# One 16 KB read for two 8 KB reads in the stores of full slots

## The chip, the cores and the metric

The kernel runs on one core of one Trainium2 chip. The metric is the device time of one execution in microseconds, taken as the median of several runs; before the change it is 323.96 us (three runs, 323.84 to 323.97).

## The reference

There are 128 examples x[b], each a float32 matrix of 128 rows (c) by 1024 columns (t), and eight 128 x 128 weight matrices. Each example picks one matrix by its subject number, is multiplied by it, and the product is added to the example:

```python
def _L0_cond_ref(x, subjects, weights):
    w = weights[subjects]                      # (128, 128, 128)
    out = jnp.einsum('bct,bcd->bdt', x, w)     # (128, 128, 1024)
    return out
x = x + _L0_cond_ref(x, itok_B_0_7, L0_cond_weights)
```

The input and the output have 67.1 MB each, so that the kernel has to move 134.2 MB between DRAM and SBUF.

## The kernel before

Four examples (G = 2 times H = 2) make one *slot* of 2 MB: in SBUF a slot is 16 KB on each of the 128 partitions, four rows of 4 KB that stand side by side. There are 32 slots of work (NT = 32) and room for 12 of them in SBUF (SLOTS = 12); slot i of the work uses place i mod 12. Two examples, half a slot, are the unit of computing: 64 halves in all.

*Loads.* The ACT queue issues them (L188 to L195): four of 512 KB for each slot, one for each example. On the DRAM side a load takes pieces of 16 KB (ROWS = 4 rows of 4 KB), and on the SBUF side it fills one 4 KB row on each partition. From the thirteenth slot on, ACT first waits at L193 until the stores of the slot that had the same place before have landed.

*Computing.* For each half, POOL copies the two weight matrices that the subjects choose into small tiles (L222), once both loads of the half have landed (the wait at L226). PE makes eight matmuls of 512 columns (L156), and DVE adds the two products, which lie in PSUM, to the two examples in place (L234): the result stands where the input was.

*Stores.* SP issues them (`store`, L140 to L147) after it has waited for the addition of the half (L239). Slot 0 and slot 31 are stored by halves (1 MB each; of the last half one example alone, 512 KB), the thirty slots between them whole, 2 MB in one DMA. The very last example, 512 KB, is stored at L252 by an ordinary DMA, which SP issues last. On the DRAM side a store writes pieces of 4 KB, one row of an example. On the SBUF side a piece is `g` rows: in the kernel before, `g = min(G, q1 - q0)`, so that a whole slot is read in two pieces of 8 KB from each partition.

Loads and stores are in two hardware queues (the profile's q10 for the loads, q1 for the stores, which also has the two small loads at the start) that share the same 16 DMA engines. Each DMA of 128 partitions is spread over all 16. In the trace each queue's work is a row of packets: one for each contiguous piece that is read, and at the end of a DMA one of 4 bytes on each engine, which counts up the DMA's semaphore.

Of the kernel before, what the change touches and what calls it, by code (L numbers as in the profile page):

```python
# [30 lines left out]
G = 2  # L31
# [20 lines left out]
def transfer(nc, engine, out, in_):  # L52

    later, nc._always_lower_symbolic_ap = nc._always_lower_symbolic_ap, False
    ins, outs = engine.lower_ap_dma(in_), engine.lower_ap_dma(out)
    nc._always_lower_symbolic_ap = later
    return engine.add_instruction(
        mybir.InstDMACopy(  # L60
            name=nc.get_next_instruction_name(),
            engine=engine.engine,
            ins=ins,
            outs=outs,
            mode="Copy",
            cce_op=ALU.bypass,
            queue=QUEUES[engine.engine],
        )
    )
# [3 lines left out]
def kernel(  # L73
# [17 lines left out]
    if room:  # L91
        sbuf("room", C, room // 4)
    x_all = sbuf("x_all", C, SLOTS * H * G * T)
    xs = [
        x_all[:, i * H * G * T : (i + 1) * H * G * T].rearrange("c (q t) -> c q t", t=T)
        for i in range(SLOTS)
    ]
# [42 lines left out]
    def store(i, q0, q1):  # L140
        k, b = i % SLOTS, i * H * G
        transfer(
            nc,
            nc.sync,
            out[b + q0 : b + q1].rearrange("g d t -> d g t"),
            xs[k][:, q0:q1, :].rearrange("d (o g) t -> d o (g t)", g=min(G, q1 - q0)),
        ).then_inc(s_first if i == 0 and q1 == G else s_pair[k][(q1 - 1) // G], DMA)  # L147

    def multiply(slot, q0, q1):
# [15 lines left out]
    with tc.tile_critical():  # L165
# [22 lines left out]
        for i in range(NT):  # L188
            k = i % SLOTS
# [8 lines left out]
        for j in range(NT * H):  # L198
            i, q0, q1 = j // H, j % H * G, (j % H + 1) * G
            k = i % SLOTS  # L200
# [37 lines left out]
            if i == 0 or q1 == H * G or i == NT - 1:  # L238
                nc.sync.wait_ge(s_added, j + 1)  # L239
                store(i, q0 if i in (0, NT - 1) else 0, q1 - (b == B - 1))  # L240
# [46 lines left out]
```

## Time and profile before

| what | value |
|---|---|
| median of three runs | 323.96 us |
| the profiled execution's own time | 324.29 us |
| span of that execution, first to last instruction | 322.5 us |
| PE busy | 241.0 us (75%) |
| DVE busy | 147.9 us (46%) |
| POOL busy | 34.0 us (11%) |
| end of the last addition (L234) in the span | 274.8 us |
| moved by the DMA engines | 134.79 MB, mean 418 GB/s |

The busy times are sums over the whole span. No computing engine is busy for more than three quarters of it, and the last addition ends 47.7 us ahead of the span's end. The span and the execution's own time differ by 1.8 us, which lie around the first and the last instruction.

### The profile page before, as it was taken

How to read it: one execution, taken by the hardware profiler on the slowest of the kernel's cores; microseconds unless marked ns; L12 is line 12 of the kernel's file. 1: busy time of each engine (PE TensorE's matmuls, PEld its weight loads, DVE VectorE, ACT ScalarE, POOL GpSimd, SP SyncE). 2: the span in 40 equal slices, each digit the busy share in tenths (PEclk: the TensorE clock that was granted, in tenths of full speed). 3: DMA queues.
4: the chain of work that ended last, by engine and by line, in shares of the span. 5: the costliest groups of instructions: out<-in, count | busy, mean ns of one | idle time of the engine just before them, and what ended most of it. 6: DMA issues, size and time to landing. Idle time of an engine off the chain costs nothing. (4 is left out here: it accounts for less than half of the span.)

```text
span 322.5 us, 2012 instructions
## 1 busy us (share of the span) xinstructions
PE 241.0 (75%) x518; PEld 94.8 (29%) x518; DVE 147.9 (46%) x68; POOL 34.0 (11%) x132
## 2 busy tenths in 40 slices
PE   6999999988988888888888898888887687000000
PEld 2344444333333333333333333333332232000000
DVE  1266665655555555545555555555553554000000
POOL 0011111111111111111111111111111010000000
PEclk9799999999999999999999999999999999655555
DMA  7999999999999999999999999999999999999997
GB/s 240 431 414 431 417 426 434 429 416 429 426 426 426 434 418 428 431 422 426 431 425 424 431 419 428 429 426 424 431 422 424 430 422 427 427 425 427 426 429 296
DMA packets 16070, 134.79 MB, mean 418 GB/s; under 512 B 2625, under 2 KB 3650, under 8 KB 3906
## 3 DMA queue, kind: packets, MB, share of 16 engines
q1 hardware_dynamic: 9922, 67.64, 50.0%
q10 hardware_dynamic: 6144, 67.12, 49.6%
q14 instruction: 4, 0.03, 0.0%
HBM read 67.63 MB, written 67.11 MB: 418 GB/s over the span
## 5 line engine op out<-in xcount | busy, mean ns | idle before, releaser
L156 PE MATMUL ps<-x_all,w 128*128 (+1 forms) x512 | 235.9, 607 | 29.8 <-PEq L152 29.8
L234 DVE TENSOR_TENSOR x_all<-ps,x_all 128x2048 f32<-128x2048 f32 x64 | 146.7, 2292 | 125.1 <-PE ps L156 125.1
L156 PEld LDWEIGHTS ps<-x_all,w 128*128 128x128 f32 x512 | 92.9, 191 | 173.1 <-issue 173.1
L222 POOL COPY w<-w_all 128x128 f32 x128 | 33.8, 293 | 234.2 <-DMA x_all<-in_x_dram 186.2
L173 PE MATMUL ps<-zeros 128*128 128x512 f32 x6 | 5.1, 1020 | 1.7 <-DVE zeros L170 1.7
L173 PEld LDWEIGHTS ps<-zeros 128*128 128x128 f32 x6 | 1.9, 330 | 3.7 <-issue 2.1
L170 DVE MEMSET zeros<- 128x512 f32 x1 | 0.5, 485 | 1.1 <-SPq L165 1.1
L180 DVE TENSOR_SCALAR near<-given 1x128 int32<-1x128 int32 x1 | 0.2, 215 | 0.6 <-DMA given<-in_itok_B_dram 0.6
L184 DVE CUSTOM_DVE_ANT_0 index<-near,wrap 1x256 uint16<-1x256 uint16 x1 | 0.3, 278 | 0.0
L182 DVE TENSOR_SCALAR wrap<-near 1x128 int32<-1x128 int32 x1 | 0.2, 216 | 0.0
L274 POOL MEMSET const-float32-0.0<- 128x1 f32 x1 | 0.1, 98 | 0.2 <-issue 0.2
L274 POOL MEMSET const-bfloat16-1.0<- 128x1 bf16 x1 | 0.1, 101 | 0.0
L274 POOL MEMSET const-uint8-127<- 128x1 uint8 x1 | 0.1, 101 | 0.0
L274 POOL MEMSET const-float32-1.0<- 128x1 f32 x1 | 0.1, 98 | 0.0
## 6 DMA issues: line engine op xcount, KB each, us to landing
x_all<-in_x_dram ACTq DMA_DIRECT2D x128, 512.0 KB, 32.0
out_dram<-x_all SPq DMA_DIRECT2D x30, 2048.0 KB, 48.3
out_dram<-x_all SPq DMA_DIRECT2D x3, 1024.0 KB, 13.5
out_dram<-x_all SPq DMA_DIRECT2D x2, 512.0 KB, 20.6
w_all<-in_L_cond_weights_dram SPq DMA_DIRECT2D x1, 512.0 KB, 6.1
given<-in_itok_B_dram SPq DMA_DIRECT2D x1, 0.5 KB
```

The lines of the kernel that those rows point to most:

```text
L156: mm = nc.tensor.matmul(p[:, q % G, t : t + N], ws[q % W_SLOTS][:, 0, :], x_all[:, bass.ds(at, N)], start=True, stop=True,)
L170: nc.vector.memset(zeros, 0.0).then_inc(s_zeros, 1)
L173: nc.tensor.matmul(ps[P_SLOTS - 1][:, G - 1, :N], zeros[:, :D], zeros, start=True, stop=True)
L180: nc.vector.tensor_scalar(near, given, -S, S - 1, ALU.max, ALU.min).then_inc(s_index, 1)
L182: nc.vector.tensor_scalar(wrap, near, 0, S, ALU.is_lt, ALU.mult).then_inc(s_index, 1)
L184: nc.vector.tensor_tensor(index, near, wrap, ALU.add).then_inc(s_index, 1)
L222: copy = nc.gpsimd.tensor_copy(ws[b % W_SLOTS], w_all[:, bass.ds(subject[b % R], 1), :])
L234: nc.vector.tensor_tensor(mine, p, mine, ALU.add).then_inc(s_added, 1)
L274: nc = _bacc.Bacc("TRN2", target_bir_lowering=False, num_devices=1)
```

## The change

One argument in `store` is changed. Where a store covers a whole slot, q1 - q0 is 4, and the four rows of a partition are now read as one piece of 16 KB; the stores by halves (q1 - q0 = 2) and of one example keep their pieces. The bytes, their order, the 4 KB pieces on the DRAM side, the number of DMAs, the semaphores and the waits stay as they are, and every engine's instructions stand in the same order as before.

```diff
@@ def store(i, q0, q1)
             nc.sync,
             out[b + q0 : b + q1].rearrange("g d t -> d g t"),
-            xs[k][:, q0:q1, :].rearrange("d (o g) t -> d o (g t)", g=min(G, q1 - q0)),
+            xs[k][:, q0:q1, :].rearrange("d (o g) t -> d o (g t)", g=q1 - q0),
         ).then_inc(s_first if i == 0 and q1 == G else s_pair[k][(q1 - 1) // G], DMA)
```

## The prediction

> **What bounds the kernel now.** I read the page's slices first, to find the resource that is full; then its queues; then the DMA view cut to three stretches, to see what one packet costs and how the two queues share the engines; then the end of the timeline. The profile's page:
>
> ```profile
> PE   6999999988988888888888898888887687000000
> ...
> DMA  7999999999999999999999999999999999999997
> ...
> q1 hardware_dynamic: 9922, 67.64, 50.0%
> q10 hardware_dynamic: 6144, 67.12, 49.6%
> ...
> out_dram<-x_all SPq DMA_DIRECT2D x30, 2048.0 KB, 48.3
> ```
>
> The DMA engines are full in every slice but the first and the last; PE stops near slice 34. So the time is that of the bytes. The counts tell what a packet is. A load of 512 KB puts 32 KB on each of 16 engines: two pieces of 16 KB and the 4-byte packet, 3 packets, and 128 x 16 x 3 = 6144. A full slot's store puts 128 KB on an engine: 16 pieces of 8 KB and one of 4 bytes, 17 packets. A store needs 48.3 us to land: the store queue has a backlog.
>
> The three stretches are 10 to 18 us (loads alone), 40 to 240 us (both) and 270 to 315 us (stores alone); columns are packets, MB, share of 16 engines.
>
> ```profile
> DMA packets 309, 3.42 MB, mean 428 GB/s; under 512 B 100, under 2 KB 100, under 8 KB 100
> ...
> q10 hardware_dynamic: 309, 3.42, 100.8%
> ...
> DMA packets 9180, 85.27 MB, mean 426 GB/s; under 512 B 1791, under 2 KB 1791, under 8 KB 1791
> ...
> q10 hardware_dynamic: 4538, 49.47, 58.5%
> q1 hardware_dynamic: 4638, 35.77, 42.5%
> ...
> DMA packets 2489, 19.19 MB, mean 426 GB/s; under 512 B 147, under 2 KB 147, under 8 KB 147
> ...
> q1 hardware_dynamic: 2489, 19.19, 101.3%
> ```
>
> Two things are to be seen. Loads alone, both together and stores alone all run at 426 to 428 GB/s. And while both queues have work they get the same number of packets (4538 and 4638), not of bytes: the engines take turns by packet, and the 4-byte packet takes a turn too. Three turns of loads carry 32 KB, 10.7 KB a turn; 17 turns of stores carry 128 KB, 7.5 KB a turn. That makes 1.42; the bytes above stand 1.38 to 1. So loads run ahead of stores until the 12 places are full, and this lead is stored at the end, long after computing is over:
>
> ```profile
> 267.95 0.53 POOL L222 COPY w<-w_all 128x128 f32 x2 [3.48 <-DMA x_all<-in_x_dram]
> ...
> 272.50 2.29 DVE L234 TENSOR_TENSOR x_all<-ps,x_all 128x2048 f32<-128x2048 f32 x1 [1.67 <-PE ps L156]
> ...
> 301.87 0.37 SPq L252 DMA_DIRECT2D out_dram<-x_all  x1
> ```
>
> The waits of SP's queue (total us, times, longest) have the rest:
>
> ```profile
> SPq L283 <- DMA out_dram<-x_all: 19.2, 1, 19.2
> ```
>
> The last load has landed at 267.9; the half's last addition ends at 274.79, 6.84 us after its weight copy begins at 267.95; SP still has DMAs to wait for at the end, 19.2 us. The computing of the last slot costs nothing now, because from 267.4 us on, where the last load packet ends, the engines still have 54 us of stores to move, 23 MB at 426 GB/s.
>
> **What the change does, part by part.**
>
> *Fewer packets.* The 30 full stores go from 16 to 8 pieces on an engine: 30 x 8 = 240 packets fewer for each engine, 3840 in all. What is one worth? By duration: in the middle stretch a load packet of 16 KB takes (58.5% of 3200 us, less 1519 small ones of 9 ns) / 3019 = 615.5 ns, a store packet of 8 KB (42.5% of 3200 us, less 272 small ones) / 4366 = 310.9 ns; two of these less one of those is 6.3 ns, and 240 x 6.3 = 1.5 us. But durations overlap (the shares are over 100%), so I also take the pace. The semaphore steps of the loads that land from 9.10 to 18.94 us, eight of them, are 1.230 us apart on the mean engine, or 615 ns for 16 KB with its part of the 4-byte packets. Those of the full stores that land alone are 4.918 us apart, 614.7 ns for 16 KB. By that a saving is 0; with 9 ns taken off for each small packet it is 613.6 - 610.5 = 3.1 ns, or 0.75 us. Below nothing: no row has a 16 KB read from SBUF; the slowest stretch of mixed traffic, 245 to 267 us, ran at 423 GB/s for 426, and 63 MB at that pace would be 1.0 us longer. Bounds: 1.0 us lost to 1.5 us gained. I take 0.4 us gained, the middle of the two readings of pace, since these count what passes, not how long a packet is in flight.
>
> The Trainium skill (DMA: Bandwidth & Descriptors, "Why small descriptors are slow (HBM only)") puts some 3 cycles of fixed cost on each packet. By its 850 MHz that is an estimated 3.5 ns, 0.85 us here; the paces above lie below that, and by the page the sum below would be 0.45 us smaller.
>
> *The turns.* A full store is now 9 packets for 128 KB, 14.2 KB a turn, against the loads' 10.7. Where both have work, stores get 57% of 426 GB/s, 244, and loads 183. Stores can't outrun computing, so the store queue runs empty now and then, and loads take what is left: in balance each slot takes 2 x 2.097 MB / 0.426 = 9.84 us, of which its store needs 2.097 / 0.244 = 8.6 us. The early backlog (computing starts at 7.05 us a slot) shrinks by 1.2 us a slot and is gone well before slot 30. The engines stay full: the load queue has work as long as places are free, and the lead is then some 4 to 6 MB of the 25 that 12 places hold. PE's rate is no bound (eight matmuls take 3.7 us, a half is due each 4.9 us).
>
> *The end.* Now the last loads come late, with little left to store over the computing. Let C be the start of the last weight copies; the last load packet ended 0.52 us before (267.43 to 267.95). Slot 30 had its copy 9.84 us earlier, its addition ended 6.84 us after that, and its store's first packet comes 3.85 us after the issue, as that of the first store (16.46 to 20.31 us): at C + 0.88. So at C - 0.52 slots 30 and 31 are wholly unstored, 4.19 MB; slot 29, a slot earlier, finishes 8.6 us after its first packet, at C - 0.4. With no hole, 4.19 MB take 9.83 us, to C + 9.31. But the chain of the last half is longer: addition done at C + 6.84, issue 0.03 later; that issue takes 0.6 us and L252's follows 0.73 us after; the first packet of a DMA in an idle queue comes 1.32 us after its issue (the first load: 0.92 to 2.24), so L252's at C + 9.5; 512 KB take 1.23 us: C + 10.75. The hole is 1.44 us. Bounds: if slot 30's store starts after 1.3 us, 0.27 MB less lie over it and the hole is 2.1 us; each 0.43 MB of leftover backlog makes it 1 us less, and 0.6 MB close it: 0 to 2.1 us. I take 1.44.
>
> Sum: 1.44 - 0.4 = +1.0 us. On the profiled execution's 324.29 us (span 322.5 and 1.8 around it) that is 325.3; it lay 0.33 above the median, so on 323.96 it is 325.0 us.
>
> **The rivals.**
>
> *Faster: a piece is worth its duration and the shares don't move.* If the 1.38 to 1 is no matter of packets but of something that the change leaves alone, the lead and the 47 us of stores at the end remain, the last slot stays covered, and the whole gain is that of the packets: up to 1.5 us, 322.5. It counts as faster from 2.7 ns a pair (0.65 / 240). For it: the sum of durations. Against it: the equal packet counts, and the pace. Chance 0.15.
>
> *No visible change.* The same fixed shares with 0.4 us of gain: 323.6; or the piece is cut in two again when the DMA is laid out, then q1 keeps 9922 packets and the time 323.96. Against the last: loads read 16 KB pieces already. Chance 0.20.
>
> The Trainium skill (DMA: Bandwidth & Descriptors, "Queues, rings and completion order") has an engine drain a packet of some 9 to 17 descriptors from one queue before it turns to the next. A load's 3 would then be one turn of 32 KB and a store's 17 one of up to 128 KB, before and after: this rival. The rows above disagree: loads got more bytes, not a quarter.
>
> *Slower by far.* If the last two stores also need 3.85 us to their first packet, L252's begins at C + 12.0 and the hole is 4.0 us: +3.6, 327.6. Against it: the first store waited behind a full queue of loads, and at the end there are none. Chance 0.07.
>
> **How the numbers follow.** Forecast 0.58: 325.0, with its own range of 324.0 to 326.1 (hole 0.8 to 2.1, gain 0.75 to 0). A measurement of this kernel tells about 0.2%, 0.65 us, from no change. Of the forecast's chance some 0.07 lies below that and counts as the same: slower 0.51 + 0.07 = 0.58, same 0.20 + 0.07 = 0.27, faster 0.15. The range goes from 323.1, which takes in no change and half of the faster rival's ground, to 326.5: what is outside is the far end of that rival and the far slower one.
>
> **What will show it.** q1 has 9922 - 3840 = 6082 packets. In the middle, loads and stores move the same bytes, 213 GB/s each, and PE waits for loads from early on. A full store lands some 15 us after its issue, for 48.3. The last weight copies begin near 312 us for 267.95, the last addition ends near 318, and SP's last wait is near 3 us for 19.2. The last slice or two show a hole in the DMA engines. I am wrong if the lead still grows through the span, if the DMA rate in the middle leaves 425 to 429 GB/s, or if the engines stay full to the last microsecond.

## The result, and the profile after

The changed kernel is slower. Measured first, it took 326.44 us (median of five runs, 324.99 to 326.65) against 323.94: a ratio of 1.0061, with a 95% interval of 1.005 to 1.0072. In a second measurement, of twelve runs, it took 324.91 us against 323.96: 1.0028, interval 1.0011 to 1.0045. The two medians differ because the changed kernel has three levels and nothing between them. Of all its 22 runs, those that were made for a trace among them, 5 lie at 323.65 to 324.05, 12 at 324.80 to 325.33 and 5 at 326.44 to 326.73; their median is 325.0. The kernel before has one level (323.80 to 324.38 in the 23 runs of the second measurement).

The profiled execution took 324.99 us, so it shows the middle level. Its page, lines as those shown of before:

```profile
PE   7999959598787976768886978768678788779670
...
DMA  7999999999999999999999999999999999999995
...
q1 hardware_dynamic: 6082, 67.64, 49.5%
q10 hardware_dynamic: 6144, 67.12, 49.5%
...
out_dram<-x_all SPq DMA_DIRECT2D x30, 2048.0 KB, 13.2
```

The store queue q1 has 3840 packets fewer, as it must. The DMA engines are as full as before up to the last slice. But PE now works up to the last slice but one, with gaps between, and a full store lands 13.2 us after its issue, for 48.3: there is no backlog of stores any more. The stretch from 40 to 240 us (packets, MB, share of 16 engines) shows why:

```profile
DMA packets 6800, 85.32 MB, mean 427 GB/s; under 512 B 1591, under 2 KB 1591, under 8 KB 1591
...
q1 hardware_dynamic: 2978, 43.55, 51.2%
q10 hardware_dynamic: 3818, 41.74, 49.4%
```

The rate is the same (427 GB/s for 426), but the stores now move as much as the loads, where they had 35.77 MB to 49.47. The store queue has fewer packets than the load queue because it is empty part of the time: for 23.2 of these 200 us no packet of a store is under way, for 0.1 us in the kernel before. The end of the timeline, SP's last wait, and the DMA view from 310.1 us on, where the last 16 KB packet of the loads ends (one digit is 0.33 us):

```profile
308.22 10.33 SPq L59 DMA_DIRECT2D out_dram<-x_all  x3
...
311.19 0.53 POOL L222 COPY w<-w_all 128x128 f32 x2 [5.62 <-DMA x_all<-in_x_dram]
...
315.75 2.29 DVE L234 TENSOR_TENSOR x_all<-ps,x_all 128x2048 f32<-128x2048 f32 x1 [3.82 <-PE ps L156]
...
319.27 0.37 SPq L252 DMA_DIRECT2D out_dram<-x_all  x1
```

```profile
SPq L283 <- DMA out_dram<-x_all: 2.5, 1, 2.5
```

```profile
DMA  9995959798989798999994210004999999910000
...
q1 hardware_dynamic: 572, 4.03, 72.8%
```

When the last load ends, 4.03 MB are left to store, and the DMA engines run dry for over a microsecond, in the digits 22 to 28, 317.0 to 319.3 us, between the store of slot 31's first half and the last two stores. Those wait for the last addition, which ends at 318.04.

### The profile page after: what moved, and what is told of

Same layout as the page of the kernel before. It is cut to its first block, busy times and chain, and to the rows that moved or that the text cites. A ratio compares the mean times of both kernels' runs of the same rounds, so it can differ in the third digit from the quotient of the medians.

```text
span 323.2 us, 2012 instructions
## 1 busy us (share of the span) xinstructions
PE 251.2 (78%) x518; PEld 98.6 (31%) x518; DVE 147.9 (46%) x68; POOL 34.3 (11%) x132
## 5 line engine op out<-in xcount | busy, mean ns | idle before, releaser
L156 PE MATMUL ps<-x_all,w 128*128 (+1 forms) x512 | 245.7, 628 | 62.9 <-PEq L152 62.1
L156 PEld LDWEIGHTS ps<-x_all,w 128*128 128x128 f32 x512 | 96.8, 198 | 212.5 <-issue 212.4
## 6 DMA issues: line engine op xcount, KB each, us to landing
out_dram<-x_all SPq DMA_DIRECT2D x30, 2048.0 KB, 13.2
```

Of the source, the lines that this page charges most:

```text
L156: mm = nc.tensor.matmul(p[:, q % G, t : t + N], ws[q % W_SLOTS][:, 0, :], x_all[:, bass.ds(at, N)], start=True, stop=True,)
```

## The experiments

Two theories stood against each other. *Bare chain*: the queues take turns by packet; with 9 packets in a full store for 17, stores keep up with the loads, the lead is lost, and the computing of the last half has too little to hide behind. *Pieces*: a 16 KB read from SBUF is itself slower, at least at times.

**The change again.** No edit; twelve runs and a trace.

> The changed kernel once more, to see whether its two levels (325.0 and 326.5 us) come back on one chip and which stretch of the span differs between them. Turns (the two queues take turns by packet, so that the lead of the loads is lost and the last slot's computing lies bare): the middle runs at 426 to 428 GB/s at either level, and the difference lies in the last 15 us, where the hole in the DMA engines is 1.5 us at the lower level and some 3 us at the upper. Pieces (a 16 KB read from SBUF passes more slowly at times): the rate in the middle is lower by 0.5% at the upper level and the hole is the same.

324.91 us, with runs at all three levels: 4 runs at 323.65 to 324.05, 6 at 324.8 to 325.14, 2 at 326.47 to 326.73. The traced run was at the middle one again (325.14 us): 427 GB/s in the middle, 4.00 MB unstored at the end of the last load. What differs at the uppermost level it could not show.

**Smaller loads, stores as before.** The sharing is turned round by the loads alone; no store piece is changed. In the kernel before:

```diff
-ROWS = 4
+ROWS = 2
```

> The stores of before, in 8 KB pieces; the loads in 8 KB pieces for 16 KB. A load is then 5 packets for 32 KB, 6.4 KB a turn, against the stores' 7.5: stores get ahead without a single 16 KB read from SBUF. Turns: as the changed kernel, the last weight copies near 311 us, a hole of 1.4 to 3 us near 318, time 325.0 to 326.7. Pieces: no 16 KB store piece, so the time of before, 323.9, or less than 0.5 above it for the smaller loads, and the last copies near 268 us.

325.93 us (325.86 to 326.14 in five runs), ratio 1.0062, interval 1.0049 to 1.0075. Its last weight copies begin at 312.05 us. The stretch from 40 to 240 us and the SP wait:

```profile
q1 hardware_dynamic: 5554, 42.88, 50.9%
q10 hardware_dynamic: 6435, 42.21, 50.4%
```

```profile
SPq L283 <- DMA out_dram<-x_all: 2.5, 1, 2.5
```

Equal bytes, no backlog, and the loss, without one 16 KB read from SBUF. Pieces can't explain that. At the end of the last load 3.86 MB are unstored, and the last packet comes 2.24 us after the point at which the engines would have been done with no gap, as in the changed kernel (2.30; 1.09 in the kernel before). Of this kernel's loss of 1.97 us the end has 1.15. Another 0.2 us lie in the middle: between 40 and 280 us it moves 102.17 MB, the kernel before 102.27. The rest was not followed.

**Small pieces for the late slots.** 16 KB pieces in 19 stores, 8 KB from slot 20 on.

```diff
-            xs[k][:, q0:q1, :].rearrange("d (o g) t -> d o (g t)", g=q1 - q0),
+            xs[k][:, q0:q1, :].rearrange("d (o g) t -> d o (g t)", g=q1 - q0 if i < 20 else min(G, q1 - q0)),
```

> The stores of slots 1 to 19 in 16 KB pieces, those of slots 20 to 30 in 8 KB pieces. Turns: from slot 20 on loads gain 74 GB/s again, so that some 10 MB of stores lie over the last slot's computing; no hole, and what is left is the gain of the fewer packets, 0 to 0.5 us: 323.4 to 324.0. Pieces: 19 of 30 stores still have what makes the changed kernel slower: +0.7 to +1.6, 324.6 to 325.5.

323.97 us in eleven runs (323.69 to 324.25), ratio 0.9998, interval 0.9989 to 1.0007. The levels are gone, and so is the loss:

```profile
DMA  7999999999999999999999999999999999999997
...
SPq L283 <- DMA out_dram<-x_all: 16.1, 1, 16.1
```

SP again waits 16.1 us at the end, for stores that lay over the last addition (10.26 MB unstored at the last load). The 19 stores in 16 KB pieces cost nothing that shows in the time, and gain nothing that shows in it.

**Larger loads, stores as changed.** The other way to give the loads their lead back, in the changed kernel:

```diff
-ROWS = 4
+ROWS = 8
```

> The stores of the changed kernel, and the loads in 32 KB pieces for 16 KB: a load is 2 packets for 32 KB, 16 KB a turn, against the stores' 14.2. Turns: loads are ahead again, by some 25 GB/s, so that the lead grows to 8 to 12 MB by the end; no hole, time 323.2 to 324.0. Pieces: all 16 KB store pieces are there, 325.0 to 326.5.

The time is not as expected: 333.74 us (331.70 to 339.93 in six runs), ratio 1.028, interval 1.0249 to 1.0311. The sharing and the end are: 13.45 MB are unstored at the last load, and SP's last wait is 19.2 us again. In the stretch from 40 to 240 us, where both queues always have work, the packets are equal to within three, and the loads lead by 25 GB/s:

```profile
q10 hardware_dynamic: 2759, 45.16, 53.4%
q1 hardware_dynamic: 2756, 40.07, 47.2%
```

Of the 16 KB stores 2444 of 2447 packets end within 6 ns after a packet of the loads has started, so that the queues do change places after every packet. Without the 4-byte packets there would be 1378 of the loads to 2447 of the stores.

The loss lies at the other end. In the DMA view from 8 to 24 us, where loads are nearly alone:

```profile
DMA packets 245, 3.97 MB, mean 248 GB/s; under 512 B 120, under 2 KB 120, under 8 KB 120
...
q10 hardware_dynamic: 240, 3.93, 95.6%
```

248 GB/s for 16 us, where the kernel before has 423 GB/s there, is 6.6 us lost: (1 - 248/423) x 16. The traced run, 332.26 us, is 8.0 us above that of the kernel before. A 32 KB load packet takes 2.03 us there (95.6% of 256 us, less 120 small packets, over 120), and 1.23 us in the middle (53.4% of 3200 us over 1378 packets). Why it is so slow with no stores beside it was not followed.

**A longer chain at the end.** Four memsets on DVE ahead of the last addition, in the changed kernel and, as a control, in the kernel before (a tile `spare` of 480 columns and a semaphore for it are declared further up).

```diff
             nc.vector.wait_ge(s_product, j + 1)
+            if j == NT * H - 1:
+                for n in range(4):
+                    nc.vector.memset(spare, 0.0).then_inc(s_spare, 1)
+                    nc.vector.wait_ge(s_spare, n + 1)
```

> The changed kernel with four memsets of 480 columns on DVE, one after the other, ahead of the very last addition: the last half's chain is some 2.2 us longer (0.46 us each and the way to a semaphore and back), nothing else moves. Bare chain: the whole 2.2 us show, 325 to 329 us for 323.7 to 326.7, at each of its levels. If the changed kernel is slower for another reason than a bare chain at the end (slower pieces in the middle): less than 0.5 us shows, since stores lie over it as before.

> The same four memsets in the kernel before. There 22.5 MB of stores lie over the last addition: 323.96, nothing shows, by either theory. It is the control for the memsets themselves.

The changed kernel: 326.14 to 329.78 us in six runs, again three levels (326.14; 327.45, 327.50, 327.58; 329.40, 329.78), each 2.3 us or more above the median of its counterpart; the last two lie above the 325 to 329 that was expected. The kernel before: 323.99 us, ratio 1.0001, interval 0.9992 to 1.001. The timeline of the lengthened changed kernel (its additions stand at L240):

```profile
315.87 0.46 DVE L238 MEMSET spare<- 128x480 f32 x1 [3.94 <-PE ps L158]
316.50 0.46 DVE L238 MEMSET spare<- 128x480 f32 x1 [0.17 <-DVE spare L238]
...
318.24 2.29 DVE L240 TENSOR_TENSOR x_all<-ps,x_all 128x2048 f32<-128x2048 f32 x1
...
321.76 0.37 SPq L258 DMA_DIRECT2D out_dram<-x_all  x1
```

From the first memset to the addition are 2.37 us; L252, here L258, is issued at 321.76 for 319.27. The whole of the added time shows where the chain is bare, and none of it where 22.7 MB of stores lie over it.

**What a level is.** Five more traced executions of the changed kernel, for traces at other levels.

> The changed kernel once more, one look, for a trace at another of its levels (323.7 to 324.0, 324.8 to 325.1, 326.5 to 326.7). Two readings. Spread: the level is how far the slowest engine lies behind the mean of the 16 when the last load lands (1.1 and 1.3 us in the two traces so far, both at the middle level): near 0 at the lowest, 2.5 or more at the highest. Amount: the level is how much is still unstored then (4.0 MB in both): 4.5 MB or more at the lowest, 3.4 or less at the highest.

> As the look before it, for one more trace: spread near 0 and 4.0 MB (spread decides) or spread 1.1 and 4.5 MB or more (amount decides) if it comes out at 323.7 to 324.0; spread 2.5 and 4.0 MB, or spread 1.1 and 3.4 MB or less, if at 326.5 to 326.7.

> The changed kernel once more, one look, for a trace at the highest level (326.4 to 326.7), which five of nineteen runs had and no trace has shown. Amount: at that level 3.4 MB or less are unstored when the last load ends. Another cause: 4.0 MB or more, and the time lies in a second hole or in the middle of the span. At 323.7 to 324.0 some 4.8 MB, at 324.8 to 325.3 some 4.0 to 4.2 MB.

> As the look before it: 3.4 MB or less unstored at 326.4 to 326.7, 4.0 to 4.2 at 324.8 to 325.3, 4.8 at 323.7 to 324.0.

> As the two looks before it: 3.4 MB or less unstored at 326.4 to 326.7, 4.0 to 4.2 at 324.8 to 325.3, 4.8 at 323.7 to 324.0.

They came out at 325.33, 323.77, 325.20, 325.03 and 325.02 us (the third to the seventh trace of the changed kernel). Together with the other traces: the end of the last 16 KB load packet, what was unstored then, and the lag, that is, how much later the last packet ended than it would have with no gap (with the unstored bytes at 426.4 GB/s).

| kernel | time, us | last load ends | unstored, MB | lag, us |
|---|---|---|---|---|
| before | 324.29 | 267.2 | 22.54 | 1.09 |
| changed, fourth trace | 323.77 | 308.3 | 4.78 | 1.11 |
| changed, third trace | 325.33 | 310.5 | 4.19 | 1.92 |
| changed, seventh trace | 325.02 | 310.1 | 4.05 | 2.30 |
| changed, first trace | 324.99 | 310.1 | 4.03 | 2.30 |
| changed, second trace | 325.14 | 310.3 | 4.00 | 2.37 |
| changed, sixth trace | 325.03 | 310.2 | 4.00 | 2.37 |
| changed, fifth trace | 325.20 | 310.3 | 3.90 | 2.60 |
| small pieces from slot 28 | 324.01 | 307.6 | 5.15 | 1.18 |

The amount decides between the two lower levels. With 4.78 MB the lag is that of the kernel before, 1.1 us, where the engines merely don't end together (their last packets end between 319.87 and 321.12 us); with 4.2 MB or less it is 0.8 to 1.5 us more. In the six traces at the middle level the last packet ends 11.74 to 11.79 us after the last load packet, whatever is unstored: that is the bare chain. In the fourth trace it is 12.33 us, so that there the stores end last and not the chain. The spread of the engines does not decide: in that trace the slowest one landed the last load 2.3 us behind the mean (309.32 to 307.06), the most of all seven. The traces also show where its 4.78 MB come from. Slot 29's store is issued at 300.09 us, 1.3 to 1.7 us later than in the other six; the store queue is empty for 3.0 us ahead of it (1.0 to 1.8 us in the others), and meanwhile the loads have the engines to themselves. What makes that store late was not followed. The DMA view of this trace, from 308.3 us on:

```profile
DMA  9989989979989989986999999489999996100000
...
q1 hardware_dynamic: 628, 4.78, 82.5%
```

One dip (the 4) is left of the hole. No trace fell on the highest level, 326.4 to 326.7, which 5 of the 22 runs have, so what it has at the end is open. Reading on along the table would ask for some 3.4 MB unstored, but that was not seen.

**Small pieces for the last three full slots alone.**

```diff
-            xs[k][:, q0:q1, :].rearrange("d (o g) t -> d o (g t)", g=q1 - q0),
+            xs[k][:, q0:q1, :].rearrange("d (o g) t -> d o (g t)", g=q1 - q0 if i < 28 else min(G, q1 - q0)),
```

> The changed kernel, with 8 KB pieces again in the stores of the last three full slots alone, 28 to 30; 27 stores keep 16 KB. Bare chain: over these three slots, some 25 us, loads gain up to 74 GB/s, 1.9 MB, so that about 6 MB are unstored at the last load, more than the 4.8 MB that cover the chain: no hole, no levels, 323.6 to 324.0 in every run. If a late switch is too short to matter, or the 16 KB pieces themselves cost time: three levels from 323.7 to 326.7 as in the changed kernel.

324.01 us (323.70 to 324.63 in eleven runs), ratio 1.0003, interval 0.9994 to 1.0012: as the kernel before, with 27 of 30 stores in 16 KB pieces. Six runs lie above the expected 324.0, four of them by 0.17 to 0.63 us, so the cover is thin here: 5.15 MB in its trace, for 6 expected. SP's last wait:

```profile
SPq L283 <- DMA out_dram<-x_all: 4.3, 1, 4.3
```

## Why the prediction was right, and where it was off

*The direction and the mechanism were right.* The turns by packet: equal bytes in the middle, no backlog, last copies at 311.19 us (forecast near 312), last addition at 318.04 (near 318), SP's last wait 2.5 us (near 3), and a hole at the end. That the queues change places after every packet, the starts of the packets show as well: between 40 and 240 us of the kernel before, 4257 of the 4366 store packets of 8 KB end within 6 ns after a load packet has started, and only 271 and 283 in the 6 ns on either side of that. Turning the sharing round by the loads alone brought the loss, giving the last slots their lead back took it away, and a longer chain showed in full. The rival of fixed shares falls with the first of these lines, and with the loads in 8 KB pieces. The Trainium skill (DMA: Bandwidth & Descriptors, "Queues, rings and completion order") has an engine drain some 9 to 17 descriptors at a turn; the traces disagree, with these changes after every packet, and with 2759 and 2756 packets for two full queues whose packets are of 32 and 16 KB.

*The end had the right net size at the level that the sum describes, in part by luck.* Forecast were 4.19 MB unstored and a hole of 1.44 us. Measured at the middle level are 3.90 to 4.19 MB, and a lag of 0.8 to 1.5 us more than before, 1.21 us in the first trace. But in the working's own measure, the chain less the time of the unstored bytes, the hole of that trace is 2.30 us (11.75 less 4.03 MB at 426.4 GB/s); that the kernel before loses 1.09 us in the same measure, because its engines don't end together, was left out of the sum, and the two errors cancel in large part. From the weight copies on the working was right: the last packet ends 10.66 us after them (311.19 to 321.85), for 10.75; a full store's first packet comes 3.89 us after its issue (298.37 to 302.26, slot 29), for 3.85. The step that was short is the one from the last load to the copies. The 0.52 us of the working run from the last closing packet of 4 bytes, and there the trace has 0.47 (310.72 to 311.19). From the last 16 KB packet, with which the 4.03 MB are counted, it is 1.09 us (310.10 to 311.19), for 0.79 in the kernel before: the closing packet ends 0.62 us after it, the time of one 16 KB store packet, where it was 0.31, that of one of 8 KB.

*The gain of fewer packets was mis-sized: 0.4 us was forecast, some 0.2 us is seen.* It shows in the traces and not in the times. Between 40 and 280 us, each packet counted by its part that lies there, the kernel before and its control with the longer chain moved 102.27 MB each, and the seven traces of the changed kernel 102.34 to 102.37; the loads in 8 KB pieces, with yet more packets, moved 102.17. The difference is worth 0.16 to 0.23 us in these 240 us. So the two readings of pace, 0 and 0.75 us, lay on either side, and their middle was too high. In the time, with 27 of 30 stores in large pieces and the hole all but closed, the ratio is 1.0003, and its interval leaves at most 0.2 us of gain. The Trainium skill (DMA: Bandwidth & Descriptors, "Why small descriptors are slow (HBM only)") would make it an estimated 0.76 us for these 27 stores (216 packets of 3.5 ns on each engine), if its packets are the pieces that are read; the interval excludes that. And the rival of durations, 1.5 us, falls with it.

*What the forecast did not have is the levels.* It worked with one amount unstored, 4.19 MB, where executions differ: 3.90 to 4.78 MB in seven traces. The sum holds for the middle level (325.0 forecast, 324.8 to 325.33 measured) and for the median of all runs, but the median of the first measurement, 326.44, lies at the highest, which the forecast's own range of 324.0 to 326.1 doesn't reach and which no experiment here explains. That the whole stated range, 323.1 to 326.5, takes it in by 0.06 us is luck.

## What to carry to other kernels

Where loads and stores filled the DMA engines together, the size of a packet set how the two queues shared them (loads to stores 1.38 to 1 with 16 and 8 KB, 1.13 to 1 with 32 and 16 KB), and so how much work was left to hide the last computing behind: count turns (all packets, the 4-byte ones too) before a piece is made larger. A kernel whose DMA engines are full for the whole span can still lose at the end; compare the work that is unstored at the last load with the chain from that load to the last store. Here 4.78 MB covered a chain of 11.75 us, and 4.2 MB did not. Favouring the loads in the last slots took the loss away; it made the kernel no faster than it was.

## What the runs showed of the hardware

A 4-byte closing packet, 9 ns long, takes a whole turn: the load queue's share follows from counting it (1.38 to 1 measured, 1.42 by the count), and it waits behind the other queue's packet (0.62 us behind one of 16 KB, 0.31 behind one of 8 KB). Loads in 32 KB pieces ran at 248 GB/s nearly alone, while loads and stores together moved 426 GB/s. And the engines don't stay together: the last load of the changed kernel landed up to 2.3 us later on the slowest engine than on the mean of the sixteen, for 0.2 us in the kernel before (267.90 to 267.72).
